# Routed experts: a chunk's tokens sorted by expert on the chip, 15 tiles of 128 places with gathered weights, in place of all experts for all tokens

## The chip, the cores and the metric

The kernel runs on one core of a Trainium2 chip. The metric is device microseconds of one execution, the median over the runs shown. The engines are PE (TensorE matmul), DVE (VectorE), ACT (ScalarE) and POOL (GpSimd); SP issues the plain DMAs. Each engine takes its instructions in the order in which they stand in its queue.

## The reference

Two layers on one sequence of 2048 tokens of width 128, all in float32. The first layer is a state-space mixer and then attention with a feed-forward part of routed experts; the second is a selective scan (Mamba) and a dense feed-forward. What bears on the change is the expert part:

```python
N_EXPERTS, TOP_K, FFN_DIM = 8, 2, 512
nx2 = _layernorm(x, ln2_w, ln2_b)                       # x: after attention
gate_logits = nx2 @ gate_W
topk_vals, topk_idx = jax.lax.top_k(gate_logits, TOP_K)
gate_w = jax.nn.softmax(topk_vals, axis=-1)
dense_gates = jnp.sum(jax.nn.one_hot(topk_idx, N_EXPERTS) * gate_w[..., None], axis=-2)
moe_out = jnp.zeros_like(nx2)
for e in range(N_EXPERTS):
    h = jax.nn.gelu(jnp.einsum('bsd,fd->bsf', nx2, fc1_w[e]) + fc1_b[e], approximate=False)
    y = jnp.einsum('bsf,df->bsd', h, fc2_w[e]) + fc2_b[e]
    moe_out = moe_out + y * dense_gates[..., e:e + 1]
```

A token's gate is zero for six of its eight experts.

## The kernel before

The 2048 tokens are four chunks of 512 (`NC = 4`, `C = 512`), a chunk being four blocks of 128 tokens (`NB = 4`). Each chunk goes through five stages: `ssd` (the state-space mixer), attention, `experts`, `scan`, `feed`. Attention of chunk c looks at all chunks up to c, so it grows from 4 to 16 key blocks for each of four groups of heads.

Attention is a coroutine (`attentions`) of two interleaved parts. `weighted` walks over the key blocks, two steps for each: a pair of score matmuls (L349), a pair that adds the row shift (L355), an exponential on ACT (L359), and the products with the values for the step pair before (L336). It has one buffer of PSUM for its scores (`ps_e`), so a step starts when ACT has read the one before. `shift` computes the row maxima that the next group's `weighted` needs: a pair of matmuls (L299) and a maximum on DVE (L309) through one other buffer (`ps_m`). There are 320 `weighted` steps in the program.

The other stages are generators that yield a weight after each piece. `with_attention` runs them, and after a piece of weight w takes attention pieces worth `w * RATE` from the coroutine. `RATE` is the sum of attention's weights over the sum of the stages' weights (`SSD`, `MOE`, `SCAN`, `FEED`), so that attention should end within `experts(2)`. The order is: `ssd(0)` with the start of `ssd(1)`, then `ssd` 1 to 3 with attention; then `experts`, `scan`, `feed` of chunks 0 and 1 and `experts(2)` with attention; then, without attention, `scan(2)` beside `experts(3)`, `scan(3)` beside `feed(2)`, and `feed(3)`. The framework's scheduler may still move instructions within this; each engine's final order is fixed when the program is built.

`experts(c)` normalizes the chunk (`nx`), transposes it (`nT`, width 512), takes the gate logits (L727), ranks the eight logits of each token by comparing all pairs (L736 to L741, `rank`), and makes a row of gates for each expert (L743 to L767). Then it loops over all eight experts: SP loads the expert's weights (`wide`, four buffers, L773 and L774); `spread_row` (L712) broadcasts the gate row; four fc1 matmuls with the 512 tokens as moving operand (L782) and four Gelu on ACT (L783); four fc2 matmuls (L787); one DVE instruction for bias and gate (L789); POOL adds the expert to `acc` (L791). At the end four PE transposes bring `acc` back (L795) and DVE adds it to the residual (L796).

ACT keeps one table at a time: `in_turn` ties the groups of exponentials and of Gelu in order, and a change between them shows as an `ACT_TABLE_LOAD`. `wide` also holds the `h1` and `h2` weights of `feed`. POOL runs elementwise work only: the power in `layernorm` (L152, L153), the sum over experts, `u * sz` in `scan` (L876), the copies of the scan's last state (L872). No DMA is issued from POOL.

Of the kernel before, what the change touches and what calls it, by code (L numbers as in the profile page):

```python
# [14 lines left out]
F32R = mybir.dt.float32r  # L15
AF = mybir.ActivationFunctionType
# [3 lines left out]
P = 128  # L20
T = 2048
D = 128
# [20 lines left out]
NF = FF // P  # L43

# [3 lines left out]
    ("bq", NG), ("bk", NG), ("fc1_b", NE * NF), ("fc2_b", NE), ("in_b", 4), ("conv_w", 8), ("conv_b", 2),  # L48
# [22 lines left out]
def two_layers(ctx: ExitStack, tc: tile.TileContext, a: dict, out: bass.AP):  # L71
# [165 lines left out]

    lows = [ap.tile([P, NB, 4, 32], F32R, name=f"lows{i}") for i in range(2)]

# [44 lines left out]
    def shift(c, g):  # L284


        qR = held[c]
        low = sp.tile([P, NB, 4], F32, tag="low", name="low")
        for r in range(NB):
            w = (r + 1) * P  # L290
            top = sp.tile([P, 4, c + 1], F32, tag="top", name="top", bufs=4)
            for kc in range(c + 1):
                diag = kc == c
                n = w if diag else C
                for i in (2, 0):
                    pss = psum("m", [P, 2, C])
                    for j in range(2):
                        hr = slice(32 * (i + j), 32 * (i + j) + 32)
                        nc.tensor.matmul(  # L299
                            pss[:, j, 0:n],  # L300
                            qR[hr, g, w - P : w],
                            kR[hr, g, kc * C : kc * C + n],
                            start=True,
                            stop=not diag,
                        )
                    yield None
                    for j in range(2 * diag):
                        nc.tensor.matmul(pss[:, j, w - P : w], ident16, mask_qk, start=False, stop=True)
                    nc.vector.tensor_reduce(top[:, i : i + 2, kc], pss[:, :, 0:n], AX.X, ALU.max)  # L309
                    yield 0.4  # L310
            nc.vector.tensor_reduce(low[:, r, :], top, AX.X, ALU.max, negate=True)
        lw = lows[g % 2]
        nc.vector.tensor_copy(lw[:, :, :, 0], low)
        nc.vector.tensor_tensor(lw[:, :, :, 1], low, lw[:, :, :, 0].bitcast(F32), ALU.subtract)
        pm = psum("m", [P, C])
        for r in range(NB):
            nc.tensor.matmul(
                pm[:, r * P : (r + 1) * P], lw[:, r].rearrange("p i r -> p (i r)"), identR, start=True, stop=True
            )
        sh = ak.tile([P, C], F32R, tag="sh", name="sh")  # L320
        nc.vector.tensor_copy(sh, pm)  # L321
        held[c, g] = sh
# [73 lines left out]

    def in_step(main, other, ratio=1.0):
# [50 lines left out]
    SSD, MOE, SCAN, FEED = 43.0, 62.0, 46.0, 40.0  # L448
# [241 lines left out]

    halo1 = wp.tile([P, 2, 3], F32, name="halo1")
# [8 lines left out]
    for n in (NE, DS):  # L700
# [14 lines left out]
    def experts(c, z):  # L715
        yield from after_stage(("attention", c))
        x = xc[c]
# [24 lines left out]
        top = sp.tile([P, NB], F32, tag="etop", name="etop")  # L742
        nc.vector.tensor_reduce(top, lg, AX.X, ALU.max)  # L743
        ge = sp.tile([P, NB, NE], F32, tag="ge", name="ge")
        nc.vector.tensor_tensor(ge, lg, top.unsqueeze(2).to_broadcast([P, NB, NE]), ALU.subtract)
        nc.scalar.activation(ge, ge, AF.Exp)
        nc.vector.scalar_tensor_tensor(ge, rank, 1.5, ge, ALU.is_lt, ALU.mult)
        nc.vector.tensor_reduce(top, ge, AX.X, ALU.add)
        nc.vector.reciprocal(top, top)
        ge2 = sp.tile([P, NB, 2, NE], F32, tag="ge2", name="ge2")  # L750
        for i in range(2):
            nc.vector.tensor_tensor(ge2[:, :, i], ge, top.unsqueeze(2).to_broadcast([P, NB, NE]), ALU.mult)
        pgt = z.bank([2 * NE, C])
        for b in range(NB):
            nc.tensor.matmul(
                pgt[:, b * P : (b + 1) * P],
                ge2[:, b].rearrange("p i e -> p (i e)"),
                ident,
                start=b == 0,
                stop=True,  # L760
                skip_group_check=b > 0,
            )
        gT = rows_in[NE][0]
        ghi = z.line("ghi", (2 * NE, C), F32R)
        nc.vector.tensor_copy(ghi, pgt)
        nc.tensor.matmul(pgt, minus_low[NE], ghi, start=False, stop=True, skip_group_check=True)
        nc.vector.tensor_copy(gT[0 : 2 * NE], pgt)  # L767
        yield 1.5

        acc = z.line("acc")  # L770
        for e in range(NE):
            we = z.tile("wide", [P, 2, FF], 4)
            nc.sync.dma_start(we[:, 0], a["fc1"][e])  # L773
            nc.sync.dma_start(we[:, 1].rearrange("p (k d) -> p k d", k=NF), a["fc2"][e].rearrange("(k p) d -> p k d", p=P))  # L774
            pg = z.bank([P, C])
            spread_row(pg, NE, gT, e)
            gb = z.line("gb")
            nc.vector.tensor_copy(gb, pg)
            hs = [z.four("h") for _ in range(2)]
            for f in range(NF):  # L780
                ph = z.bank([P, C])
                nc.tensor.matmul(ph, we[:, 0, f * P : (f + 1) * P], nT, start=True, stop=True)  # L782
                in_turn("gelu", nc.scalar.activation(hs[f // 2][:, f % 2, :], ph, AF.Gelu, bias=col("fc1_b", e * NF + f)))  # L783
            yield 3.7
            py = z.sum([P, C])
            for f in range(NF):
                nc.tensor.matmul(py, we[:, 1, f * P : (f + 1) * P], hs[f // 2][:, f % 2, :], start=f == 0, stop=f == NF - 1)  # L787
            dst = acc if e == 0 else z.line("ye")
            nc.vector.scalar_tensor_tensor(dst, py, col("fc2_b", e), gb, ALU.add, ALU.mult)  # L789
            if e:  # L790
                nc.gpsimd.tensor_tensor(acc, acc, dst, ALU.add)  # L791
            yield 3.5
        pt = z.bank([P, NB, D])
        for b in range(NB):
            nc.tensor.transpose(pt[:, b, :], acc[:, b * P : (b + 1) * P], ident)  # L795
        nc.vector.tensor_tensor(x, x, pt, ALU.add)  # L796
# [88 lines left out]
    def feed(c, z):  # L885
# [16 lines left out]
        for name, scale in (("h1", "h1_s"), ("h2", "h2_s")):  # L902
            w = []
            for i in range(2):
                w.append(z.tile("wide", [P, 2, FF], 4))
# [24 lines left out]
    def second_layers():  # L930
        for c in range(2):
            yield from experts(c, side)
            yield from scan(c, side)
            yield from feed(c, side)
        yield from experts(2, side)
# [4 lines left out]
    with tc.tile_pool(name="work2", bufs=2, side="right") as pool:  # L940
        other = Stream(pool, 9, 5, ("m", "e"), "o")
        together((scan(2, side), SCAN), (experts(3, other), MOE))
# [6 lines left out]
def _layout(L0_attn_u, **w):  # L949
# [7 lines left out]
    def per_pair(v):  # L957
# [11 lines left out]
    w_dt1[2 * DS :] = w["L1_attn_dt_proj_w"]  # L969
    col = {  # L970
# [9 lines left out]
        "fc1_b": cols(w["L0_ffn_fc1_b"]),  # L980
        "fc2_b": cols(w["L0_ffn_fc2_b"]),
# [37 lines left out]
        "fc1": w["L0_ffn_fc1_w"].transpose(0, 2, 1),  # L1019
        "fc2": w["L0_ffn_fc2_w"].transpose(0, 2, 1),  # L1020
# [25 lines left out]
```

## Time and profile before

| | |
|---|---|
| median of 3 runs | 1773.75 us (1770.18 to 1774.82) |
| profiled execution | 1789.77 us, its span 1788.1 us |
| mean granted TensorE clock in it | 0.886 |
| PE, DVE, ACT, POOL busy | 88%, 54%, 40%, 10% of the span |
| DMA | 32.54 MB in all, mean 18 GB/s |
| `experts(0)`, `(1)`, `(2)` with attention | 446 to 611, 866 to 1043, 1296 to 1464 us |
| `scan(2)` beside `experts(3)` | 1464 to 1617 us |

Durations below are from the profiled execution. Busy PE time is modelled (a matmul's span includes its way through the array, and neighbours overlap), so the pace of a group of matmuls is read from the distance between starts. In the timeline a line is a merged group: start, length, engine, source line, operation, output<-inputs, shapes, count, and in brackets the idle time before it with what ended it. In the groups, `| busy us, mean ns | idle before` stands at the end.

### The profile page before, as it was taken

To read this page: it belongs to the slowest core of one execution; us is meant where nothing else is said; L and a number is where in the kernel's file an instruction comes from. 1 tells how busy PE (TensorE), PEld (TensorE's weight loads), DVE (VectorE), ACT (ScalarE), POOL (GpSimd) and SP (SyncE) were. 2 spreads that over 40 slices of the span, in tenths; PEclk is the share of its full clock that TensorE was granted. 3 is DMA by queue.
4 is the path that set the end of the run, shared out by engine and by line. 5 is a ranking of instruction groups with operands and counts; after the bars stand their busy time and mean duration, and the time that the engine had idled before them with its cause. 6 is when DMAs were issued, how large, how long until landed. Compare 5 with 4: busy or idle time off the path is not lost.

```text
span 1788.1 us, 16822 instructions
## 1 busy us (share of the span) xinstructions
PE 1580.7 (88%) x6630; PEld 668.3 (37%) x6630; DVE 968.5 (54%) x1565; ACT 715.3 (40%) x837; POOL 186.3 (10%) x256
## 2 busy tenths in 40 slices
PE   6898999998999878789999988889998888988978
PEld 3554545445333323233433322233333233333334
DVE  5466546646344568853545458873441035675860
ACT  2222232322545353435355454434544525543522
POOL 3322111211000100010000000010000010111010
PEclk9797897967999889989789888999888888998989
DMA  2000000002000000001001000000100020110000
GB/s 83 1 1 1 1 1 1 1 1 82 24 24 24 24 0 1 0 1 30 24 24 36 24 12 1 1 1 24 30 24 21 15 83 24 35 36 1 0 6 6
DMA packets 34384, 32.54 MB, mean 18 GB/s; under 512 B 2385, under 2 KB 25089, under 8 KB 34305
## 3 DMA queue, kind: packets, MB, share of 16 engines
q1 hardware_dynamic: 33872, 30.41, 5.7%
q8 instruction: 52, 0.85, 0.2%
q10 hardware_dynamic: 432, 1.06, 0.2%
q14 instruction: 28, 0.22, 0.0%
HBM read 30.41 MB, written 1.05 MB: 18 GB/s over the span
## 4 chain that ended last, share of the span: by engine, by line
PE 63%; DVE 21%; ACT 7%; issue 5%; POOL 2%; DMA 1%; SPq 0%; POOLq 0%; DVEq 0%; ACTq 0%
DVE hs L867 8%; PE ps_o L336 8%; PE ps_a L782 6%; PE ps_m L299 5%; PE ps_c L787 5%; PE ps_e L349 5%; DVE top L309 4%; PE ps_a L911 3%; PE ps_e L355 3%; DVE db L864 3%; PE ps_a L870 2%; ACT probs L359 2%; PE ps_a L563 2%; PE ps_c L588 2%; PE ps_a L546 1%
## 5 line engine op out<-in xcount | busy, mean ns | idle before, releaser
L309 DVE TENSOR_REDUCE top<-ps_m 128x2 f32<-128x1024 f32 (+3 forms) x320 | 339.8, 1062 | 276.4 <-PE ps_m L299 153.3
L359 ACT ACTIVATE probs<-ps_e 128x1024 f32<-128x1024 f32 (+3 forms) x320 | 286.6, 896 | 456.7 <-PE ps_e L355 254.2
L299 PE MATMUL ps_m<-kR,qR 32*128 32x512 f32 (+3 forms) x640 | 177.6, 501 | 43.9 <-DVE top L309 36.9
L349 PE MATMUL ps_e<-qR,kR 32*128 32x512 f32 (+3 forms) x640 | 168.7, 503 | 24.0 <-ACT probs L359 23.3
L867 DVE TENSOR_TENSOR_SCAN hs<-da,hlast,db 128x512 f32<-128x512 f32 x128 | 160.2, 1286 | 31.1 <-ACT da L862 27.8
L336 PE MATMUL ps_o<-probs,vv 128*9 128x512 f32 (+3 forms) x1152 | 168.4, 588 | 0.6 <-ACT probs L359 0.5
L299 PEld LDWEIGHTS ps_m<-kR,qR 32*128 32x128 f32 x640 | 73.8, 200 | 208.3 <-DVE top L309 112.1
L355 PE MATMUL ps_e<-sh,onesR 32*128 32x512 f32 (+3 forms) x640 | 143.2, 418 | 0.8 <-DVE sh L321 0.8
L870 PE MATMUL ps_a<-hs,ident 128*128 128x512 f32 x192 | 111.6, 668 | 29.6 <-DVE hs L867 27.5
L349 PEld LDWEIGHTS ps_e<-qR,kR 32*128 32x128 f32 x640 | 66.6, 196 | 175.0 <-ACT probs L359 94.6
L782 PE MATMUL ps_a<-nT,wide 128*128 128x512 f32 x192 | 117.5, 725 | 6.3 <-ACT h L783 5.9
L862 ACT ACTIVATE da<-dl 128x1024 f32<-128x1024 f32 x64 | 66.7, 1054 | 83.5 <-PE ps_a L870 55.7
L787 PE MATMUL ps_c<-h,wide 128*128 128x512 f32 x192 | 97.8, 629 | 0.0
L791 POOL TENSOR_TENSOR acc<-acc,ye 128x512 f32<-128x512 f32 x28 | 37.3, 1332 | 511.8 <-DVE ye L789 511.8
L783 ACT ACTIVATE h<-ps_a,cols 128x512 f32<-128x512 f32 x96 | 64.2, 686 | 52.1 <-PE ps_a L782 51.8
L355 PEld LDWEIGHTS ps_e<-sh,onesR 32*128 32x128 f32 x640 | 71.7, 207 | 4.3 <-issue 2.8
L789 DVE SCALAR_TENSOR_TENSOR ye<-ps_c,cols,gb 128x512 f32<-128x512 f32 x21 | 15.8, 750 | 101.6 <-PE ps_c L787 101.4
L870 PEld LDWEIGHTS ps_a<-hs,ident 128*128 128x128 f32 x192 | 29.8, 194 | 87.2 <-DVE hs L867 81.4
L864 DVE TENSOR_TENSOR db<-du,ps_c 128x1024 f32<-128x1024 f32 x48 | 58.3, 1216 | 6.3 <-PE ps_c L712 3.9
L782 PEld LDWEIGHTS ps_a<-nT,wide 128*128 128x128 f32 x192 | 38.8, 225 | 44.4 <-issue 21.7
L359 ACT ACT_TABLE_LOAD x39 | 50.0, 1283 | 12.1 <-PE ps_e L355 11.4
L911 PE MATMUL ps_a<-g,wide 128*128 128x512 f32 x96 | 50.7, 633 | 0.0
(416 smaller groups left out, 2181.9 us busy)
## 6 DMA issues: line engine op xcount, KB each, us to landing
wide<-in_fc SPq DMA_DIRECT2D x64, 256.0 KB, 3.2
wide<-in_h SPq DMA_DIRECT2D x16, 512.0 KB, 3.6
x<-in_x SPq DMA_DIRECT2D x4, 256.0 KB, 4.9
out_x<-xn SPq DMA_DIRECT2D x4, 256.0 KB, 2.3
w<-in_w SPq DMA_DIRECT2D x3, 256.0 KB, 5.2
w_tap<-in_taps ACTq DMA_DIRECT2D x1, 576.0 KB, 7.2
rows<-in_rows ACTq DMA_DIRECT2D x1, 412.0 KB, 5.7
w_zx<-in_w_zx SPq DMA_DIRECT2D x1, 256.0 KB, 7.2
```

The lines of the kernel that those rows point to most:

```text
L299: nc.tensor.matmul(pss[:, j, 0:n], qR[hr, g, w - P : w], kR[hr, g, kc * C : kc * C + n], start=True, stop=not diag,)
L309: nc.vector.tensor_reduce(top[:, i : i + 2, kc], pss[:, :, 0:n], AX.X, ALU.max)
L336: pv = nc.tensor.matmul(o, v, prs[i // 2][:, i % 2, q0:], start=kb == 0, stop=kb == nk - 1)
L349: nc.tensor.matmul(pss[:, j, q0:], kR[hr, g, kb * P : (kb + 1) * P], qR[hr, g, q0:], start=True, stop=False)
L355: nc.tensor.matmul(pss[:, j, q0:], onesR[hr], sh[hr, q0:], start=False, stop=not diag)
L359: last = nc.scalar.activation(pr[:, :, q0:], pss[:, :, q0:], AF.Exp, scale=float(1.0 / np.sqrt(np.float32(HD))))
L782: nc.tensor.matmul(ph, we[:, 0, f * P : (f + 1) * P], nT, start=True, stop=True)
L787: nc.tensor.matmul(py, we[:, 1, f * P : (f + 1) * P], hs[f // 2][:, f % 2, :], start=f == 0, stop=f == NF - 1)
L864: nc.vector.tensor_tensor(db, du, pbn.unsqueeze(1).to_broadcast(two), ALU.mult)
L867: nc.vector.tensor_tensor_scan(hs[:, j, :], da[:, j, :], db[:, j, :], hlast[:, j, n : n + 1], ALU.mult, ALU.add)
L870: nc.tensor.matmul(py[j], ident, hs[:, j, :], start=n == 0, stop=n == DS - 1)
L911: nc.tensor.matmul(ph, w[k // 2][:, k % 2, f * P : (f + 1) * P], h[k // 2][:, k % 2, :], start=k == 0, stop=k == NF - 1)
```

## The change

A new coroutine `route(c)` takes the gate part. From the ranks it marks the two chosen experts of each token, counts by two small matmuls with `upto` and `ones` how many tokens of each expert stand before a token, rounds every expert's count up to whole tiles of 128, and so gives each token two places among `TILES = 15` tiles of 128. The normalized rows are scattered to these places in a DRAM buffer (`sorted_x`) by eight indirect DMAs from POOL, one for each choice and block; and for every tile the row numbers of its expert's weights are computed (`weights`).

`experts(c)` then loops over the 15 tiles: SP loads four tiles of sorted rows at a time (`xt`), PE transposes them; for each tile POOL gathers 128 rows of 1156 floats (fc1, fc2, both biases: 592 KB) by index into `wide`; four fc1 matmuls with 128 columns, four Gelu of 128 columns, for two tiles in turn; four fc2 matmuls with the hidden part as stationary operand; DVE adds the bias and SP writes the tile to `sorted_y`. At the end POOL gathers the two results of each token by eight indirect DMAs (`both`), and eight DVE instructions add them, times the gates, to the residual.

`MOE` goes from 62 to 34, which also raises `RATE`. `route(0)` runs before `experts(0)`; `route(1)` and `route(2)` beside `feed(0)` and `feed(1)`; `route(3)` ahead of `experts(3)` in its thread. `lows` has one buffer instead of two, and the fc biases are no longer in `cols`.

```diff
+TOP = 2
+TILES = C * TOP // P + NE - 1
+WIDE = FF + NF * D + NF + D
-    lows = [ap.tile([P, NB, 4, 32], F32R, name=f"lows{i}") for i in range(2)]
+    lows = [ap.tile([P, NB, 4, 32], F32R, name="lows")]
-    SSD, MOE, SCAN, FEED = 43.0, 62.0, 46.0, 40.0
+    SSD, MOE, SCAN, FEED = 43.0, 34.0, 46.0, 40.0
+    sorted_x = [tc.dram_tile([TILES * P, D], F32, name=f"sorted_x{i}") for i in range(2)]
+    sorted_y = [tc.dram_tile([TILES * P, D], F32, name=f"sorted_y{i}") for i in range(2)]
...
+    for i in range(2):
+        for n in range(0, TILES, NB):
+            w = min(NB, TILES - n)
+            nc.sync.dma_start(sorted_x[i][n * P : (n + w) * P]..., zeros[:, 0 : w * D]...)
...
+    def route(c, z):
+        yield from after_stage(("attention", c))
...
+        chosen = sp.tile([P, NB, NE], F32, tag="chosen", name="chosen", bufs=1)
+        nc.vector.tensor_scalar(chosen, rank, TOP - 0.5, None, ALU.is_lt)
+        pn = z.bank([P, 2, NB, NE])
+        for i, m in enumerate((upto, ones)):
+            nc.tensor.matmul(pn[:, i]..., m, chosen..., start=True, stop=True)
...
+        places = sp.tile([P, TOP * NB], U32, tag="places", name="places")
+        nc.vector.tensor_copy(places, picked[:, 0].rearrange("p k b -> p (k b)"))
+        xs, ys = sorted_x[c % 2], sorted_y[c % 2]
+        for k in range(TOP):
+            for b in range(NB):
+                i = k * NB + b
+                nc.gpsimd.indirect_dma_start(
+                    xs[:, :], bass.IndirectOffsetOnAxis(ap=places[:, i : i + 1], axis=0), nx[:, b, :], None
+                )
...
+    def experts(c, z):
...
+        for n in range(0, TILES, NB):
+            w = min(NB, TILES - n)
+            xt = z.line("xt")
+            nc.sync.dma_start(xt[:, 0 : w * D]..., xs[n * P : (n + w) * P]...)
+            pt = z.bank([P, C])
+            for i in range(w):
+                nc.tensor.transpose(pt[:, i * P : (i + 1) * P], xt[:, i * D : (i + 1) * D], ident)
+            nT = z.line("xT")
+            nc.vector.tensor_scalar(nT[:, 0 : w * P], pt[:, 0 : w * P], col("ln2_w"), col("ln2_b"), ALU.mult, ALU.add)
+            for two in range(0, w, 2):
+                held_h = []
+                for i in range(two, min(two + 2, w)):
+                    we = z.tile("wide", [P, WIDE], 4)
+                    nc.gpsimd.indirect_dma_start(
+                        we, None, a["experts"], bass.IndirectOffsetOnAxis(ap=weights[:, n + i : n + i + 1], axis=0)
+                    )
+                    ph = z.bank([P, C])
+                    h = z.line("h")
+                    for f in range(NF):
+                        part = slice(f * P, (f + 1) * P)
+                        nc.tensor.matmul(ph[:, part], we[:, part], nT[:, i * P : (i + 1) * P], start=True, stop=True)
+                    for f in range(NF):
+                        part = slice(f * P, (f + 1) * P)
+                        in_turn("gelu", nc.scalar.activation(h[:, part], ph[:, part], AF.Gelu, bias=fc1_b[:, f : f + 1]))
+                    held_h.append((i, we, h))
+                yield 2.0
+                for i, we, h in held_h:
+                    py = z.sum([P, D])
+                    for f in range(NF):
+                        nc.tensor.matmul(py, h[:, f * P : (f + 1) * P], we[:, FF + f * D : FF + (f + 1) * D], ...)
+                    y = z.tile("y", [P, D], 3)
+                    nc.vector.tensor_tensor(y, py, we[:, FF + NF * D + NF :], ALU.add)
+                    nc.sync.dma_start(ys[(n + i) * P : (n + i + 1) * P], y)
+                yield 2.0
+        both = z.four("both")
+        for k in range(TOP):
+            for b in range(NB):
+                i = k * NB + b
+                nc.gpsimd.indirect_dma_start(
+                    both[:, k, b * D : (b + 1) * D], None, ys[:, :], bass.IndirectOffsetOnAxis(ap=places[:, i : i + 1], axis=0)
+                )
+        for k in range(TOP):
+            for b in range(NB):
+                nc.vector.scalar_tensor_tensor(
+                    x[:, b, :], both[:, k, b * D : (b + 1) * D], gate[:, k, b : b + 1], x[:, b, :], ALU.mult, ALU.add
+                )
+        yield 1.0
...
     def second_layers():
+        yield from route(0, side)
         for c in range(2):
             yield from experts(c, side)
             yield from scan(c, side)
-            yield from feed(c, side)
+            yield from beside(feed(c, side), route(c + 1, side))
         yield from experts(2, side)
...
-        together((scan(2, side), SCAN), (experts(3, other), MOE))
+        together((scan(2, side), SCAN), (chain(route(3, other), experts(3, other)), MOE))
```

## The prediction

> **What bounds the kernel now.** I read the page's totals, the chain and the groups first, then the windows of the stages that change, then single rows of the timeline.
>
> ```profile
> PE 1580.7 (88%) x6630; PEld 668.3 (37%) x6630; DVE 968.5 (54%) x1565; ACT 715.3 (40%) x837; POOL 186.3 (10%) x256
> PE 63%; DVE 21%; ACT 7%; issue 5%; POOL 2%; DMA 1%; SPq 0%; POOLq 0%; DVEq 0%; ACTq 0%
> L782 PE MATMUL ps_a<-nT,wide 128*128 128x512 f32 x192 | 117.5, 725 | 6.3 <-ACT h L783 5.9
> L787 PE MATMUL ps_c<-h,wide 128*128 128x512 f32 x192 | 97.8, 629 | 0.0
> ```
>
> PE carries the chain, POOL and DMA nearly nothing of it. The expert matmuls wait for little: their time is PE content. The windows (stretch, length, then busy PE, PEld, DVE, ACT, POOL with counts, granted clock, DMA share, GB/s) of `experts(0)`, `(1)`, `(2)` and of `scan(2)` beside `experts(3)`:
>
> ```profile
> 446.00:611.00 165.00, 157.13 (x673) 62.41 (x669) 73.67 (x102) 79.57 (x93) 10.15 (x8) 0.92 0.09 26
> 866.00:1043.00 177.00, 166.00 (x753) 64.34 (x751) 85.11 (x121) 86.25 (x97) 12.39 (x11) 0.87 0.08 24
> 1296.00:1464.00 168.00, 145.64 (x601) 56.25 (x601) 33.59 (x56) 79.37 (x91) 10.17 (x8) 0.84 0.12 38
> 1464.00:1617.00 153.00, 127.91 (x290) 50.47 (x290) 100.23 (x144) 70.69 (x78) 22.25 (x32) 0.92 0.10 28
> ```
>
> In the first three PE is the limit; in the last, DVE (100 of 153 us) shares it, so a PE saving is not paid out there in full. A `weighted` step by itself, and two matmul groups of `feed(3)`:
>
> ```profile
> 1393.60 0.50 PE L349 MATMUL ps_e<-qR,kR 32*128 32x512 f32 x2 [0.20 <-ACT probs L359]
> 1394.43 1.02 ACT L359 ACTIVATE probs<-ps_e 128x1024 f32<-128x1024 f32 x1 [0.88 <-PE ps_e L355]
> 1395.51 0.50 PE L349 MATMUL ps_e<-qR,kR 32*128 32x512 f32 x2 [1.18 <-ACT probs L359]
> 1774.91 3.60 PE L911 MATMUL ps_m<-g,wide 128*128 128x512 f32 x8
> 1778.34 4.11 PE L921 MATMUL ps_o<-w,g 128*128 128x128 f32 x32
> ```
>
> A step takes 1.91 us from start to start. A 512-column fp32 instruction takes (1778.34−1774.91)/8 = 0.429 us, a 128-column one 4.11/32 = 0.128; each fp32 matmul is two instructions.
>
> **PE content.** Removed per chunk: 8 experts × 16 instructions × 0.429 = 54.9; eight broadcasts of a gate row and the old transposes, gates' rows and logits that go, about 5.6 (a broadcast between 0.2 and 0.56; I take 0.3, since neighbours overlap). Together 60.5. Added: 15 tiles × 16 × 0.128 = 30.8; 15 transposes at 0.15 (four of L163 in 0.60) = 2.3; counting 0.5. Together 33.6. So a chunk saves 27, not the factor of four by which arithmetic falls: 1920 places against 4096, but at narrower tiles.
>
> **The stages.** `RATE` rises from 1.189 to 1.424. Counting L349 pairs in the order of both built programs, `experts(0)`, `(1)`, `(2)` hold 35, 40, 41 steps before and 31, 34.5, 34 after; 16.5 move into `ssd` (+9) and `scan`/`feed` (+7.5). A serial model, steps × 1.91 + expert PE, gives 127, 137, 139 before (sum 403) against 165, 177, 168 measured (510). After it gives 93, 99, 98 (291). If the excess is proportional (510/403 = 1.27), 368 come out, −142; if the excess of 107 is fixed (both kernels make eight Gelu groups a chunk, so the table changes of 1.28 us stay), 398, −112. I take the middle, **−127**. ACT does not undo this: 60 short Gelu for 32 long ones, estimated at 0.32 each (between 0.686 for 128x512 and 0.23 for a 128x32 row), 19 against 22.
>
> **Moved steps.** In `ssd` PE is 96% busy at 0.81 clock, so a step costs its PE content, 1.46/0.81 = 1.8; elsewhere 1.91. 16.5 × 1.85 = **+31**.
>
> **The scatter before experts(0).** No DMA is issued from POOL in this trace. POOL's hold per indirect DMA is bounded by its rows L152 (0.235 us) and L876 (2.345); I take 1.2, nearest L153 (1.04) and L791 (1.33) (both whole elementwise passes). The landing is bounded by
>
> ```profile
> w_eg<-in_w_eg SPq DMA_DIRECT2D x1, 4.0 KB, 1.6
> out_x<-xn SPq DMA_DIRECT2D x4, 256.0 KB, 2.3
> wide<-in_h SPq DMA_DIRECT2D x16, 512.0 KB, 3.6
> ```
>
> and I take 2.3. In the built order every scatter waits for the one before to land, since they write one DRAM tile: 8 × 3.5 = 28. With some 17 small DVE operations ahead (3 us), two L309 in front of them (2.5), and the load of `xt` (3.2), the transposes of `xt` come 37 after the gate; two steps and some `shift` pieces, 5 us, stand before them in PE's queue. PE is in order, so all attention behind waits: **+32**, between 15 (a scatter at 1.8) and 50 (at 6). Routes 1 and 2 lie beside `feed`, with over 20 steps (42 us) before their `xt`: nothing, while that cover holds; else another 32 each. Filling the buffers with zeros is SP work in `ssd`: nothing.
>
> **The combine at each chunk's end.** Last y add 0.2, its write 2.7, eight gathers at 1.2 on POOL, one landing 2.3, then the adds and the layernorm (3.5): 18.4, against 6.1 before. DVE is in order, so the first add of `both` holds the L309 behind it, and PE follows. Cover is 5 steps for chunks 0 and 1, leaving +7 each; none for chunk 2, +12: **+26**, between 10 (hold 0.5) and 60 (hold 2.345 with each step's cover lost).
>
> **The tail.** `scan(2)` beside `experts(3)` goes in 16 rounds of 5.75 us; after, DVE (3.7) and PE (3.5) per round would allow about 4.2: −20. Against it stand the scatters of `route(3)` (they end 3 us after the loop of the scan starts), four tiles ahead of the first round (8), the longer combine (12), and u*sz (L876) queued behind gathers on POOL: **0**, ±20.
>
> **Weight gathers.** 592 KB each, 60 of them, four buffers. They are issued at least 8 us before fc1 wants them, and 512 KB land in 3.6: nothing, because the three tiles before cover them; uncovered, 4 us a tile. On POOL a gather that waits for its buffer holds the small POOL work of `layernorm` behind it; I put no price on that beyond the range.
>
> **Clock.** After PE waits 3.11 us, the next 16 narrow instructions run at 0.217 each, at the granted clock of the second line:
>
> ```profile
> 1613.08 3.47 PE L880 MATMUL ps_c<-w_out,u 128*128 128x128 f32 x16 [3.11 <-POOL u L876]
> 1613.00:1617.00 4.00, 3.91 (x20) 3.67 (x20) 1.53 (x5) 0.00 (x0) 2.53 (x4) 0.61 0.00 0
> ```
>
> Some four new long waits at 1.5 us lost: **+6**. The Trainium skill ("TensorE: Matmul & The Clock Gate", Part 1) says that an idle window of about 3.4 us halves the clock and about 3.4 us of busy time restores it; by it each wait costs 1.7, 6.8 in place of 6.
>
> A rule that speaks against the change is in "DMA: Bandwidth & Descriptors", Anatomy of one DMA: a DMA by GpSimd's path takes 2.0 us plus bytes/436e3. By it a 64 KB scatter takes 2.15 and the chain 17 us in place of 28 (the sum would be 11 lower), while a 592 KB gather takes 3.4; no row here shows either.
>
> **Sum.** −127 + 31 + 32 + 26 + 0 + 6 = −32 on the profiled 1789.8 (span 1788.1 and 1.7 around it): 1757.8. The median stands at 0.991 of that execution: **1742 us**.
>
> **Rivals.**
> 1. *POOL becomes the bound in the serial places (slower).* About 38 holds are uncovered: 8 scatters, 24 gathers of three combines, and six in the tail. Break-even is 1.2 + 32/38 = 2.0 us a hold. At the longest POOL row, 2.345, the sum is 1789.8 − 32 + 44, or 1785 by the median; at 3.2 (if POOL were held as long as a 256 KB weight load takes) 1817. For: no row shows such a hold, and its addresses are made from an index per row. Against: POOL is 10% busy.
> 2. *Narrow matmuls stay at the slow pace (slower; the change doesn't deliver).* If fc1 and fc2 take 0.217 as in L880, 240 × 0.089 = 21 per chunk come back, 64 in three: 1805. It decides from 0.17 an instruction. For: a weight load for every 128 columns (PEld of L782 0.225 by itself) and more waits. Against: L921 does 0.128.
> 3. *Cheap routing (faster).* Scatters at 2.0, holds at 0.5, and the proportional −142: −142 + 31 + 20 + 10 − 10 + 4 = −87, which is 1687.
>
> **How the numbers follow.** Forecast 0.48 (0.44 of it faster), rival 3 0.13, rival 1 0.24 (0.22 slower), rival 2 0.12 (0.11 slower), and 0.03 for worse sums of them. A difference of 0.3% is about what a measurement of this kernel can tell (its runs span 0.26%). So faster 0.57, same 0.07, slower 0.36. All unknowns at their good ends give about 1670, all at the bad ones 1834; the range, 1680 to 1815, takes in rival 3, rival 2 and nearly all of rival 1. The forecast's own range is 1715 to 1768.
>
> **What would show it.** Right: a PE wait of about 32 us at the `xt` transposes before `experts(0)`, released by a DMA; DVE waits of some 10 us at an add of `both` in each chunk; `experts(0)` to `(2)` at 118 to 140 us each without these; fc1 and fc2 near 0.128 from start to start; a scatter every 3.5 us; the first tail stage still near 153. Wrong: scatters or gathers of `both` 2 us or more apart on POOL (rival 1), fc near 0.2 (rival 2), or fc1 waiting for `wide`, which I cost at nothing.

## Result: slower by 0.7%, and the profile after

The changed kernel takes 1787.64 us (median of 7 runs, 1783.58 to 1796.53); its ratio to the kernel before is 1.0071, 95% interval 1.0048 to 1.0094. The forecast was 1742, range 1680 to 1815. The time lies in the range, but on the other side of no change. The profiled execution took 1796.53 us with a span of 1793.9, 5.8 more than before. Both profiled executions were longer than the medians, the one before by more (16 us against 9), so the profiles differ by less than the medians do.

First the totals, the granted clock in 40 slices, and the chain's shares of the changed kernel:

```profile
span 1793.9 us, 18362 instructions
PE 1506.4 (84%) x7070; PEld 732.6 (41%) x7070; DVE 970.0 (54%) x1673; ACT 691.1 (39%) x946; POOL 272.1 (15%) x371
PEclk9897996886957866989999867998887766998989
PE 59%; DVE 18%; ACT 7%; issue 7%; POOL 5%; DMA 3%; SPq 0%; POOLq 0%; DVEq 0%; ACTq 0%
```

Two readings carry the result. PE is busy for 74 us less (1580.7 to 1506.4) but idle for 80 us more (1788.1 − 1580.7 = 207.4 before, 287.5 now). And the mean granted clock fell from 0.886 to 0.833. That mean also covers idle time. In these traces the clock is granted either in full or at half, and PE was busy at the half clock for 371 us before and 477 us after, and idle at it for 36 and 122 us. An estimate, if an instruction at the half clock takes twice as long: counted in time at the full clock, PE's work fell by 127 us (1395 to 1268), the half clock took 53 us of that back and the waits 80, which gives the 6 us that the profile is longer. The same reckoning finds the known edits of e12 and e13 below: 58 us of the 61 added and 82 of the 82 taken away.

By stage (ends read from the trace: last add to x in `ssd`, last add of an expert stage, `out_x` issued by `feed`; steps are L349 pairs before, L355 pairs after):

| stage | before, us (steps) | after, us (steps) | difference |
|---|---|---|---|
| `ssd` | 432.6 (63) | 469.2 (74) | +36.6 |
| `experts(0)`, gate part or route(0) included | 179.0 (40) | 172.7 (32) | −6.3 |
| `scan(0)`, `feed(0)` | 250.1 (56) | 287.0 (69) | +36.9 |
| `experts(1)` | 175.8 (48) | 117.4 (35) | −58.4 |
| `scan(1)`, `feed(1)` | 249.9 (66) | 278.5 (78) | +28.6 |
| `experts(2)` | 177.1 (47) | 132.8 (32) | −44.3 |
| `scan(2)` beside `experts(3)` | 146.6 | 162.3 | +15.7 |
| the rest | 177.0 | 174.0 | −3.0 |

The expert stages did shrink, by 109 us. Everything around them grew by 115. The row of `scan(2)` ends at the last add of `experts(3)`; the last add of `scan(2)` itself came at 1617.3 us before and 1616.4 after, so to the later of the two ends this stage grew from 152.8 to 162.3, by 9.5. Of the 80 us of new waits 33 lie in `experts(0)` and 33 in this stage. Of the 53 us of half clock (the estimate above) 31 lie in the two stretches of scan and feed, whose own matmuls are the same and which have 25 more steps; the three expert stages together have 5. The windows of the three expert stages and of the first tail stage after, in the columns that the prediction explains (clock third from the right):

```profile
469.20:641.90 172.70, 128.05 (x715) 76.58 (x714) 70.61 (x144) 66.55 (x112) 31.71 (x35) 0.73 0.34 102
928.90:1046.30 117.40, 104.59 (x675) 59.55 (x675) 59.46 (x83) 69.40 (x111) 19.17 (x20) 0.90 0.32 95
1324.80:1457.60 132.80, 99.94 (x571) 60.00 (x571) 17.02 (x47) 63.77 (x106) 19.18 (x20) 0.72 0.28 84
1457.60:1619.90 162.30, 104.19 (x396) 61.15 (x396) 98.01 (x159) 63.58 (x104) 41.94 (x53) 0.77 0.28 87
```

Two of the expert stages run at 0.73 and 0.72, and the tail stage, at 0.92 before, at 0.77. The long PE waits, from the timeline (in brackets the idle time and what ended it), and POOL's scatters of chunk 0:

```profile
518.24 1.11 PE L855 MATMUL ps_a<-ident,xt 128*128 128x128 f32 x4 [24.55 <-DMA xt<-sorted_x]
1460.14 1.24 PE L169 MATMUL ps_a<-ident,xn 128*128 128x128 f32 x4 [18.95 <-DVE xn L161]
1515.76 1.09 PE L855 MATMUL ps_m<-ident,xt 128*128 128x128 f32 x4 [26.27 <-DMA xt<-sorted_x]
...
505.69 0.98 POOL L818 DMA_INDIRECT sorted_x<-xn,places  x1 [1.54 <-DMA sorted_x<-xn,places]
508.20 0.96 POOL L818 DMA_INDIRECT sorted_x<-xn,places  x1 [1.53 <-DMA sorted_x<-xn,places]
```

The first and third are the scatter chain, in front of `experts(0)` and `experts(3)`; the second is the combine of chunk 2. A scatter holds POOL for 0.96 us and the next starts 2.5 us after it, when it has landed.

### The profile page after: what moved, and what is told of

Same layout as the page of the kernel before. It is cut to its first block, busy times and chain, and to the rows that moved or that the text cites. A ratio compares the mean times of both kernels' runs of the same rounds, so it can differ in the third digit from the quotient of the medians.

```text
span 1793.9 us, 18362 instructions
## 1 busy us (share of the span) xinstructions
PE 1506.4 (84%) x7070; PEld 732.6 (41%) x7070; DVE 970.0 (54%) x1673; ACT 691.1 (39%) x946; POOL 272.1 (15%) x371
## 4 chain that ended last, share of the span: by engine, by line
PE 59%; DVE 18%; ACT 7%; issue 7%; POOL 5%; DMA 3%; SPq 0%; POOLq 0%; DVEq 0%; ACTq 0%
PE ps_o L342 8%; DVE hs L972 6%; PE ps_e L355 5%; PE ps_m L305 5%; PE ps_a L975 4%; PE ps_a L1016 4%; DVE top L315 4%; PE ps_e L361 3%; PE ps_c L879 3%; PE ps_a L870 2%; ACT probs L365 2%; DVE db L969 2%; PE ps_c L598 2%; POOL both L894 1%; PE ps_a L556 1%
## 5 line engine op out<-in xcount | busy, mean ns | idle before, releaser
L355 PE MATMUL ps_e<-qR,kR 32*128 32x512 f32 (+3 forms) x640 | 170.4, 518 | 34.8 <-ACT probs L365 32.1
L342 PE MATMUL ps_o<-probs,vv 128*9 128x512 f32 (+3 forms) x1152 | 172.7, 610 | 1.1 <-ACT probs L365 0.7
L975 PE MATMUL ps_a<-hs,ident 128*128 128x512 f32 x192 | 119.9, 728 | 26.4 <-DVE hs L972 25.7
L355 PEld LDWEIGHTS ps_e<-qR,kR 32*128 32x128 f32 x640 | 68.4, 206 | 163.1 <-ACT probs L365 99.5
L862 POOL DMA_INDIRECT wide<-in_experts,weights x60 | 59.6, 993 | 296.3 <-DVE y L887 230.9
L887 DVE TENSOR_TENSOR y<-ps_c,wide 128x128 f32<-128x128 f32 x45 | 13.0, 289 | 120.1 <-PE ps_c L879 120.0
L879 PE MATMUL ps_c<-wide,h 128*128 128x128 f32 x360 | 66.6, 333 | 5.1 <-ACT h L873 3.4
L879 PEld LDWEIGHTS ps_c<-wide,h 128*128 128x128 f32 x360 | 55.5, 230 | 25.2 <-ACT h L873 18.5
L975 PEld LDWEIGHTS ps_a<-hs,ident 128*128 128x128 f32 x192 | 34.6, 215 | 71.5 <-DVE hs L972 60.6
L870 PE MATMUL ps_a<-xT,wide 128*128 128x128 f32 x360 | 62.4, 322 | 1.1 <-DVE xT L857 1.1
L870 PEld LDWEIGHTS ps_a<-xT,wide 128*128 128x128 f32 x360 | 53.9, 226 | 12.6 <-issue 9.9
L977 POOL COPY hlast<-hs 128x2 f32<-128x2 f32 x48 | 9.0, 188 | 327.3 <-DVE hs L972 317.8
L818 POOL DMA_INDIRECT sorted_x<-xn,places x32 | 32.2, 1005 | 162.8 <-DVE whose L830 96.9
```

The costliest lines, as they stand in the source:

```text
L342: pv = nc.tensor.matmul(o, v, prs[i // 2][:, i % 2, q0:], start=kb == 0, stop=kb == nk - 1)
L355: nc.tensor.matmul(pss[:, j, q0:], kR[hr, g, kb * P : (kb + 1) * P], qR[hr, g, q0:], start=True, stop=False)
L870: nc.tensor.matmul(ph[:, part], we[:, part], nT[:, i * P : (i + 1) * P], start=True, stop=True)
L879: nc.tensor.matmul(py, h[:, f * P : (f + 1) * P], we[:, FF + f * D : FF + (f + 1) * D], start=f == 0, stop=f == NF - 1,)
L975: nc.tensor.matmul(py[j], ident, hs[:, j, :], start=n == 0, stop=n == DS - 1)
```

## Experiments

Three theories. **W**: the new waits, and the half clock that they leave, took the gain back. **N**: PE content is worth less than its time, because the granted clock falls when dense work is taken out from between attention steps. **S**: the attention steps that the higher `RATE` moves cost more in their new places than was priced. The letters R and L below are local to a run. Differences from the changed kernel are against 1787.64. The kernel before was run again with each set of runs and had medians of 1774 to 1778 us, so a difference of 4 us or less says nothing.

### e1, e2: no wait for scatters, then none for results

```diff
-  nc.sync.dma_start(xt..., xs[n * P : (n + w) * P]...)
+  nc.sync.dma_start(xt..., a["x"][n * P : (n + w) * P]...)      # e1 and e2
-  indirect_dma_start(both..., None, ys[:, :], ...)
+  indirect_dma_start(both..., None, a["x"], ...)                # e2
```

> The tiles' rows (xt) are read from the kernel's input instead of sorted_x, so PE's transposes no longer wait for the eight scatters to land; the scatters are still issued, and the experts' output is not the reference's. The profile of the changed kernel has PE waits of 24.5 us (chunk 0) and 26.3 + 3.8 us (chunk 3) there. Theory W (waits, and the half clock that each leaves behind, gave back the gain): both waits go, and with them some 15 us of half clock, so 1710 to 1735 with the mean granted clock up from 0.833 to 0.86 or more. Theory N (the narrow matmuls with a weight load each keep the granted clock low by themselves): 1730 to 1745 with the clock still at 0.83 to 0.845. Theory S (attention steps that the higher RATE moves out of the expert stages cost more than they free): the waits were partly cover for nothing else, so -55 as under N, but the stages ssd, scan + feed keep their lengths (469, 287, 279).

> As e1, and the gathers of the two results of each token read from the input as well, so they no longer wait for the writes of sorted_y; POOL still issues all eight for each chunk, and the output is not the reference's. W: a further 8 to 15 us less than e1 (the PE wait of 19 us at the end of experts(2) shrinks to what eight gathers in a row on POOL take, 10 us, of which some lies earlier), clock 0.87 or more. N: 5 to 8 us less than e1, clock unchanged. S: as N.

e1 took 1743.2 us (ratio to before 0.9827, 0.977 to 0.9883), 44 less than the changed kernel, of which the profile gives 21 in `experts(0)` (152.1 in place of 172.7) and 27 in the tail stage (135.7 in place of 162.3). Its clock rose only to 0.852 in the profile (0.838 to 0.852 over its runs), between what W and N expected. e2 took 1686.6 (0.9473, 0.9415 to 0.953), but says less than it seems: as its gathers wait for nothing, they ran at the start of each expert stage (the adds of chunk 0 ended at 510 us), and the experts' work could lie beside the scan behind it. It bounds what the dependence on the results costs, and shows no price of the combine. What it does show is that the clock stayed at 0.856 with all these waits gone (0.833 with them, 0.886 before): W explains at most a part of the clock's fall.

### e3, e4: RATE alone

```diff
-  RATE = (...) / (2.5 * SSD + 2 * (MOE + SCAN + FEED) + 0.6 * MOE)
+  RATE = (...) / (2.5 * SSD + 2 * (62.0 + SCAN + FEED) + 0.6 * 62.0)   # e3, the changed kernel
+  RATE = (...) / (2.5 * SSD + 2 * (34.0 + SCAN + FEED) + 0.6 * 34.0)   # e4, the kernel before
```

> The changed kernel with RATE of before (1.189: MOE counts 62 in RATE alone, 34 beside scan(2) as in the change). S: attention goes back to the expert stages, ssd ends near 432 instead of 469, and the sum is 15 to 40 us faster than the changed kernel (1750 to 1772). W: the same work in another place, with the same waits: within 8 us of 1788. N: the same.

> The kernel before with only RATE raised to 1.424 as in the change (no routing). S: ssd ends some 35 us later, the expert stages give back less, and the time is 1790 to 1810. W and N: attention is PE work wherever it lies, so 1765 to 1785.

e3 took 1814.2 (1.020, 1.0156 to 1.0243), e4 1815.9 (1.018, 1.0103 to 1.0256); both are slower than any of the theories had put them. e3 goes against S as it was put, but not cleanly: at the low rate 56 steps were left over after `experts(2)` and ran by themselves. They tell something else. The window of attention alone:

```profile
1320.00:1480.00 160.00, 128.87 (x542) 41.39 (x542) 47.21 (x65) 69.26 (x70) 2.54 (x3) 0.61 0.00 1
```

PE is recorded busy for 81% of it, and the granted clock is 0.61. Attention by itself does not hold the clock: the 56 steps start between 1320 and 1487 us, 3.0 us a step, not the 1.91 of my one row. e4 ended attention before `experts(2)`, so its total mixes things too; but its `ssd` is 469.5 us with 74 steps, where the kernel before has 432.6 with 63, and nothing else of the change is in it.

### e5: no routing beside feed

```diff
-  yield from beside(feed(c, side), route(c + 1, side))
+  yield from feed(c, side)                      # experts(1), (2) use the routes of chunk 0
```

> route(1) and route(2) are left out beside feed(0) and feed(1); experts(1) and experts(2) use the places, weights and sorted rows of chunk 0 (so the output is not the reference's); route(0), route(3) and all the rest stay. Prediction's step (routing beside feed costs nothing because 22 to 24 attention steps cover it): 1778 to 1792. Rival R (routing work takes PE's and DVE's places in the queue and leaves a lower clock; scan + feed are 287 and 279 us long, where the kernel before has 250 and 13 and 12 steps fewer, which at 2.0 are only 25 each): 20 to 30 us faster than the changed kernel, 1755 to 1768.

1785.0 us (1.0038, 1.0017 to 1.0058), 3 less than the changed kernel, no more than the sets differ: routing beside `feed` costs next to nothing, as predicted, and R (20 to 30) falls. The two scan and feed stretches of e5 are 275.1 and 271.6 us with 64 and 75 steps; against before, 17 more steps cost 47 us, 2.7 each.

### e6, e9: the combine without POOL

```diff
-  (eight gathers of both by POOL)
+  for k in range(TOP):
+      rows = k * C                              # e6
+      rows = (TILES - 4 * (k + 1)) * P          # e9
+      nc.sync.dma_start(both[:, k]..., ys[rows : rows + C]...)
```

> The eight gathers of POOL at each chunk's end are replaced by two plain loads by SP of 256 KB each out of sorted_y, which still wait for the last write (the rows are not those of the token, so the output is not the reference's). Rival 1 of the prediction (POOL's holds in the serial places are the price): 8 holds of 1.25 us a chunk become one transfer, 25 to 35 us faster in four chunks, 1752 to 1763. Rival L (the way write, read, layernorm is the price, whoever reads): 5 to 12 us faster, 1775 to 1783.

> e6 again, with the two plain loads by SP out of the last eight tiles of sorted_y (e6 read the first eight, which are written long before the end, so it took the wait for the last write away as well). The rows are not those of the token, so the output is not the reference's. Rival 1 (POOL's eight holds of 1.25 us in a row are the price of the combine): 25 to 40 us faster than the changed kernel, 1748 to 1763. Rival L (the way from the last y over its write to the read and the layernorm is the price, whoever reads): 5 to 12 us faster, 1775 to 1783, and most of e6's 54 us came from no longer waiting.

e6 took 1733.1 (0.973, 0.9688 to 0.9772) and its expectation was mistaken: it reads the first eight tiles and so no longer waits for the last. e9 reads the last eight and took 1777.2 (0.9995, 0.996 to 1.003), 10 less than the changed kernel. So POOL's gathers are worth about 10 us in all chunks together (L), and rival 1 of the prediction is out. The 44 us between e6 and e9 are not the wait for the last tiles alone: as in e2, the adds no longer end the stage (`experts(0)` ends after 110.7 us with 17 steps), and the last tiles could lie beside the scan behind it. They bound what the wait for the results costs.

### e7, e8, e11: cover for the waits

```diff
         routes[c] = places, weights, gate
-        yield 1.0
+        yield {0: 20.0, 3: 1.0}.get(c, 1.0)     # e7; 3: 10.0 in e8
...
         (gathers of both)
+        if c < 3:
+            yield 7.0
         (adds of both)
-    RATE = (...) / (... + 0.6 * MOE)
+    RATE = (...) / (... + 0.6 * MOE + 41.0)
```

> The reference is computed. route(0) yields 20 in place of 1 after its scatters, so about 11 attention steps stand in front of the first xt transposes in place of 4, and experts(0) to (2) yield 7 between the gathers and the adds of both; RATE falls to take this into account. W (the waits are the price): the PE wait of 24.5 us before experts(0) falls under 8 and the one of 19 us at the end of experts(2) under 8; 30 to 45 us faster than the changed kernel, 1743 to 1758. If attention only moves and each stage it leaves runs no faster (theory S): 1780 to 1792.

> As e7, and route(3) yields 10 after its scatters, so that more of scan(2) stands in front of the first xt transposes of experts(3). W: the PE waits of 26.3 and 3.8 us there shrink to under 10 and the stage beside scan(2) falls from 162 to 140 us: 15 to 25 us less than e7. If experts(3) is then what ends last there, it gives nothing or costs up to 10.

> As e8, but route(3) runs inside experts(2), between its gathers of both and the adds, so that its DVE work covers the gathers and its scatters start some 20 us earlier; experts(3) yields 5 first. The reference is computed. W: the PE waits of 18 us before scan(2) and of 11 + 11 us in the stage beside experts(3) shrink by half: 10 to 25 us less than e8, 1700 to 1715. If route(3)'s work only delays the adds: 1720 to 1735.

e7 took 1740.2 us (0.9803, 0.9748 to 0.9859) and e8 **1724.6** (0.9718, 0.9663 to 0.9774), which computes the reference and beats both kernels. In e8 the wait before `experts(0)` is gone and the one before `experts(3)` is 11 us. Cover is not all that changed: both also lower `RATE`, so `ssd` holds 68 steps in place of 74 and takes 446 and 437 us (469 in the changed kernel), and no run covers the waits at the old `RATE`. From e7 to e8 the stage beside `experts(3)` fell by only 6 us (166 to 160, where 140 had been expected); 9 of the 18 us between the two profiles lie in `ssd`, which is the same work in both. PE's waits in e8 (in total, times, longest):

```profile
PE ps_m L305 <- DVE top L315: 37.3, 46, 3.7
...
PE ps_e L169 <- DVE xn L161: 18.1, 1, 18.1
PE ps_m L855 <- DMA xt<-sorted_x: 11.3, 1, 11.3
```

The 18.1 is the combine of chunk 3, which has nothing beside it; e11's expectation had put it before `scan(2)`. e11 missed both of its ranges: 1755.3 (0.9885, 0.9833 to 0.9937), 31 more than e8. Its stage beside `experts(3)` is 171 us (160 in e8) and `experts(2)` 125.4 (118.5), so `experts(3)` gained nothing from its earlier scatters; that the routing work between gathers and adds delays the adds is the likely reason, not a measured one.

### e10: experts by themselves

```diff
-  RATE = (...) / (... + 0.6 * MOE)
+  RATE = (...) / (... + 0.6 * MOE - 54.0)       # attention ends before experts(2)
```

> RATE of the changed kernel raised once more (to about 1.67), so that attention ends before experts(2) and experts(2) runs by itself; the reference is computed. What is read is the stretch from the end of feed(1) to the end of experts(2): in e4, which left experts(2) of the kernel before alone (with its gate part), it was 83.6 us. If narrow matmuls go at 0.128 as priced: 50 to 60 us. If at 0.217 (rival 2): 70 to 85. The whole time is of less interest: 1800 to 1840 by the price of 3 us that an attention step had in ssd.

The whole took 1792.2 us (1.009, 1.0059 to 1.0122), less than expected. Without attention `experts(2)` takes 76.0 us, in the range of rival 2. In e4 the eight dense experts alone, from the first gate row to the last fc2, took 65.6 of the 83.6; here the 15 tiles, from the first xt transposes to the last fc2, take 58.6, and the combine follows. So 27 us less PE content made 7 us. Windows of e10 (the tiles) and of e4 (the dense experts with the end of the gate part):

```profile
1363.90:1420.00 56.10, 39.06 (x233) 36.57 (x234) 6.70 (x17) 15.63 (x56) 10.34 (x11) 0.71 0.48 160
```

```profile
1418.00:1491.40 73.40, 65.78 (x149) 26.81 (x149) 12.99 (x20) 23.16 (x33) 8.86 (x7) 0.94 0.19 57
```

The dense experts run at a granted clock of 0.94, the tiles at 0.71. Three lines of e10's timeline show how the tiles get there:

```profile
1382.18 1.11 PE L855 MATMUL ps_a<-ident,xt 128*128 128x128 f32 x4 [4.34 <-DMA xt<-sorted_x]
1384.20 3.78 PE L870 MATMUL ps_a<-xT,wide 128*128 128x128 f32 x16 [0.90 <-DVE xT L857]
1391.13 1.28 PE L870 MATMUL ps_a<-xT,wide 128*128 128x128 f32 x10
```

Before each group of four tiles PE waits 3 to 5 us for `xt`; then 16 instructions take 3.78 us, 0.236 each; only later in the group are they at 0.128. The load of `xt` stands in SP's queue behind the writes of the tiles before, which may be why it is late; no run separated that.

### e12, e13: PE content alone

```diff
# e12, the changed kernel
-  nc.tensor.matmul(ph[:, part], we[:, part], nT..., start=True, stop=True)
+  for _ in range(2):
+      nc.tensor.matmul(ph[:, part], we[:, part], nT..., start=True, stop=True)
# e13, the kernel before
-  for f in range(NF):
-      nc.tensor.matmul(py, we[:, 1, f * P : (f + 1) * P], hs..., start=f == 0, stop=f == NF - 1)
+  nc.tensor.matmul(py, we[:, 1, 0:P], hs[0][:, 0, :], start=True, stop=True)
```

> Each fc1 matmul of the tiles is issued twice into the same place, so the same result with 120 more 128-column instructions a chunk, 15.4 us of PE at 0.128 each. Price as predicted (x 1.27 in three chunks, little in the tail): +55 to +65, 1843 to 1853, the clock at 0.83. Theory N (the clock is low because the stream has too little dense work between attention steps): the added work lifts the granted clock of the expert stages by 0.03 or more and costs +10 to +30 only, 1798 to 1818.

> The kernel before with three of the four fc2 matmuls of each expert left out (the sum over the hidden part is cut, so the output is not the reference's); DVE, ACT, POOL, DMA and the order of attention stay. It takes 48 instructions of 0.429, 20.6 us, of PE content from each chunk (the change took about 27), and adds no wait. Price of content as the prediction had it (x 1.27 in the three stages with attention, a little in the tail): 78 to 90 us faster, 1686 to 1698. Theory N (the dense expert matmuls also hold the granted clock up beside attention; e12 got 61 us of them for 15): 15 to 45 us faster, 1732 to 1762, with the granted clock of the expert stages under 0.84.

These settle the main term. e12 adds 4 × 15.4 = 61 us of PE content and took 1802.3 (1.014, 1.0066 to 1.0214), 15 more, with the mean clock up from 0.833 to 0.855; its interval overlaps that of the changed kernel, so the 15 are not exact. e13 takes 4 × 20.6 = 82 us away, with no routing and no new wait (the one fc2 matmul that is left also needs only the first Gelu), and took 1754.2 (0.9886, 0.9832 to 0.994), 23 less than the kernel before; 11 to 30 by the interval. So a microsecond of dense PE content is worth about a quarter of a microsecond here, an eighth to a little over a third by e13's interval. The expert stages before, and then those of e13, with the steps within two of before:

```profile
432.60:611.60 179.00, 167.50 (x731) 69.66 (x733) 85.34 (x138) 81.88 (x97) 10.15 (x8) 0.90 0.15 44
861.70:1037.50 175.80, 165.41 (x743) 64.48 (x741) 84.30 (x116) 85.23 (x96) 10.18 (x8) 0.86 0.09 26
1287.40:1464.50 177.10, 151.66 (x643) 59.47 (x643) 40.71 (x65) 82.50 (x95) 10.17 (x8) 0.85 0.12 38
```

```profile
425.00:596.60 171.60, 148.60 (x662) 62.22 (x661) 84.92 (x134) 79.58 (x95) 10.18 (x8) 0.85 0.15 46
840.40:1011.90 171.50, 150.02 (x698) 60.97 (x697) 84.55 (x117) 85.00 (x96) 10.17 (x8) 0.83 0.09 27
1263.40:1432.60 169.20, 138.01 (x595) 51.98 (x595) 40.40 (x66) 82.44 (x95) 10.10 (x8) 0.79 0.13 37
```

They are 7, 4 and 8 us shorter than before, for 20.6 us less work each; the granted clock is 0.85, 0.83, 0.79, where the same stretches before have 0.90, 0.86, 0.85. In the second, PE's busy time fell by 15 (165.4 to 150.0) and its waits rose by 11.

So N is right about the price and only in part about its cause. By the estimate of the result section, e13's profile has 82 us less work, 33 us more waits and 12 us more half clock. In the three expert stages the waits rose by 28 us (47 to 76), and 19 of these are attention's score matmuls waiting for its own exponential (L359) and row maxima (L309), 25 us before and 44 in e13: where the dense work goes, attention's chain is waited for instead. In e12, 58 us more work came with 37 us less half clock and 14 us less waiting. And the price depends on the place: e12's three expert stages are as long as the changed kernel's (423.3 us in all, 422.9), while the stage beside `experts(3)`, without attention, takes 12 us more (162.3 to 174.5) for its 15.4. One profile of each shows this.

### e14, e15: steps out of ssd

```diff
-  with_attention(state_spaces(), RATE)
+  with_attention(state_spaces(), 1.189)         # e14; 1.0 on e8 in e15
-  with_attention(second_layers(), RATE)
+  with_attention(second_layers(), 1.49)         # e14; 1.40 on e8 in e15
```

> The changed kernel with the RATE of before (1.189) in the stage ssd alone, and 1.49 after it, so that attention still ends in experts(2). Some 10 steps leave ssd and lie in later stages; the reference is computed. Theory S (a step in ssd costs 3.3 us, as the lengths of ssd over all runs so far say, against 2 or less later): 8 to 20 us faster, 1768 to 1780. If a step costs the same everywhere: 1784 to 1792.

> e8 with 1.0 in ssd and 1.40 after it, so some 15 steps leave ssd. The reference is computed. S: 15 to 25 us less than e8, 1700 to 1710. Otherwise within 5 of e8's 1724.6, or slower by up to 10 since the expert stages get denser.

e14 took 1770.4 (0.9953, 0.9918 to 0.9988), 17 less than the changed kernel, as S expected: its `ssd` is 424.7 us with 63 steps. e15 took 1733.9 (0.9758, 0.9709 to 0.9807), 9 more than e8, with overlapping intervals: `ssd` fell by 30 us (406.4 with 50 steps), and the stages behind it took more than that back (131 and 131 us for `experts(1)` and `(2)`, 110 and 118.5 in e8). S holds for the eleven steps that the change moved, not for any number: in `ssd` the 13 steps from 63 down to 50 gave about 1.5 us each.

## Why the prediction was wrong

- **PE content.** The pace was right where the clock is full (ten instructions in 1.28 us, 0.128), and content fell by at least what was said: 4 × 27 = 108 us, 127 by the estimate of the result section.
- **The stages, −127: the step that failed.** It took saved PE content at its full time or at 1.27 times it (−127 is the middle of the two), as if PE time in those stages were content and nothing else. e13 and e12 price such content at 23/82 and 15/61 of itself; the 3 × 27 = 81 us would then be worth about 23, an estimate. The excess behind the factor 1.27 is neither fixed nor in proportion to content: in e13 PE's waits for attention's chain and the half clock grew when content went. With content at a quarter, the 109 us that the expert stages lost came in good part with the 36 steps that left them. How it divides between steps and content is not settled, as the two do not add.
- **Moved steps, +31: too small in count and price.** The traces show 11 more steps in `ssd` and 25 more in scan and feed (with the gate part counted into the expert stages; I had counted without it), and these stages grew by 102 us in place of 31. Over all profiles `ssd` is about 426 us with 63 steps, 443 with 68 and 463 with 74, 3.3 us a step in place of 1.8; e5 has 2.7 in scan and feed in place of 1.91. The 1.46 of PE content left out what comes with a step: `ssd` gained 18 instructions of the key and query projections (L271, L274) and 160 PE instructions in all, 32 us of work by the estimate, 2.9 a step. e14 got 17 us back by moving eleven steps.
- **The scatter before experts(0), +32.** The wait was there, released by a DMA as said, but 24.5 us: 2.5 a scatter in place of 3.5. The fit of the Trainium skill ("DMA: Bandwidth & Descriptors", Anatomy of one DMA), 2.15 us for 64 KB by GpSimd's path, was nearer than my row.
- **The tail, 0: off by 10 to 16, by where the stage is cut.** That is inside its ±20, but a wait was taken as covered that was not. The same chain stands before `experts(3)`, with PE waits of 26.3 and 3.8 us. I had set it against the loop of `scan(2)`, off the path; PE takes its instructions in order, so scan(2) waits behind the xt transposes. e1 makes the waits before `experts(0)` and `experts(3)` together worth 44 us.
- **The combine, +26.** About right for chunk 2: a PE wait of 19 us, 4 before, so +15 in place of +12; behind chunks 0 and 1 the longest PE waits are 3.1 and 3.8 us. The hold is 0.95 us. 1.2 was taken, nearest to L153, which was read as a whole pass but works on four columns. The eight gathers, 1.26 us apart, fill 10 of the 19 us, but plain loads in their place gained only 10 us in all chunks (e9). So rival 1, which needs holds of 2.0, was wrong.
- **Routing beside feed, weight gathers: nothing.** Right: e5, and PE waits for `wide` nowhere in the list of waits.
- **Clock, +6.** It was priced as four waits. By the estimate of the result section the half clock took 53 us more than before, most of it where the moved steps went. Rival 2 had the right signal (instructions at 0.236 where the clock is low), but took it for a property of narrow matmuls.
- **The rule on the clock.** The Trainium skill ("TensorE: Matmul & The Clock Gate", Part 1) lets about 3.4 us of busy time restore the clock. Here PE was recorded busy for 36 of 40 us (666 to 706 us of the changed kernel) and the clock was at 0.50 for most of it; it came back once, in the second stretch:

```profile
666.00:674.00 8.00, 7.89 (x13) 2.42 (x12) 4.45 (x6) 0.00 (x0) 0.00 (x0) 0.50 0.01 2
674.00:682.00 8.00, 7.32 (x28) 2.42 (x26) 2.32 (x3) 4.78 (x6) 0.00 (x0) 0.89 0.00 0
682.00:690.00 8.00, 5.25 (x28) 1.65 (x26) 4.76 (x6) 6.21 (x6) 0.00 (x0) 0.54 0.00 0
690.00:698.00 8.00, 7.76 (x32) 2.63 (x32) 5.39 (x6) 3.17 (x4) 0.00 (x0) 0.50 0.00 0
698.00:706.00 8.00, 7.79 (x23) 3.00 (x23) 6.19 (x7) 1.54 (x2) 0.19 (x1) 0.50 0.00 0
```

In the last two, PE was recorded busy for 15.6 of 16 us at half the clock. So "recorded busy" in a profile cannot be read as what restores the clock, and the measurement decides here. Which instructions fail to do it was not tried: the last two stretches are mostly attention steps, but the first is mostly matmuls of `scan` (L937, L952, L955).

In short: the change saved what it promised in content, this was worth about a quarter of its time, and serial chains of scatters and results that had no work beside them took more. With those covered and `RATE` lowered (e8) it is 2.8% faster than the kernel before.

## What to carry to other kernels

Before a term "less matmul work × its duration" is put on a path, look at what else runs in that stage and at what granted clock it would run alone; take a like amount of work out of the old kernel as a first experiment, which needs one edit. Count a dependent chain of DMAs at the place where an in-order engine meets its end, for every chunk, the last one too. And where a planner's weight changes, count everything that moves with a step, not the step.

## What had not been expected of the hardware

Dense matmuls cost about a quarter of their time in a kernel whose PE was recorded busy for 84 to 88% of the span, and adding 61 us of them raised the mean granted clock by 0.022. Attention by itself ran at 0.61 with PE recorded busy for 81% of the time. The length of one and the same `ssd` (74 steps) differed between profiles by 15 us, 456.0 to 470.9, with granted clocks of 0.88 and 0.84 in these two.
